# Layer 1 norms with centring and Sqrt, token columns in 4 KB runs, and a layer 3 closed in halves

## The chip, the cores and the metric

The kernel runs on one core of one Trainium2 chip. The metric is the time of one execution on the device in microseconds; it is given as the median of several runs with the lowest and the highest. The profile shows one execution: TensorE (PE, with its weight loads as PEld), VectorE (DVE), ScalarE (ACT), GpSimd (POOL), the sync engine (SP), and the DMA queues. Everything is fp32.

## The reference

The input x is a batch of B = 4 images of 64 x 64 pixels with C = 64 channels. Four layers follow each other:

```python
# layer 0: attention over the N = 4096 pixels of an image
q, k, v = x @ Wq + bq, x @ Wk + bk, x @ Wv + bv
attn = softmax(q @ k.T);  x = gamma * (attn.T @ v) + x
# layer 1: a gated convolution block, with two layer norms over the channels
y = ln(x, ln1_g, ln1_b);  y = dw3x3(y @ pw1_w + pw1_b);  y = y1 * y2      # halves of the channels
y = y * (mean(y over pixels) @ sca_w + sca_b)
x = x + (y @ pw2_w + pw2_b) * beta
z = ln(x, ln2_g, ln2_b) @ pw3_w + pw3_b;  x = x + ((z1 * z2) @ pw4_w + pw4_b) * gamma
# layer 2: attention without weights: rows h are the channels, (w, c) the 4096 tokens
x = x + softmax-weighted sum of x, scores x.T @ x
# layer 3: attention with 32 inner channels, then a batch norm over all images
y = softmax(theta(x) @ phi(x).T) @ g(x)
w_y = y @ w_W + w_b
x = x + gamma3 * (w_y - mean(w_y)) * rsqrt(var(w_y) + 1e-3) + beta3       # mean, var over b, h, w
```

The layer norm is `(x - mean) * rsqrt(var + 1e-6) * g + b` over the 64 channels of a pixel. The batch norm's mean and variance need all four images, so no output can be written before layer 3 of the last image is done.

## The kernel before

**Layout.** An image is held as a tile of 128 partitions x 2048 columns in X. The partitions are (s, c): one of two neighbouring image columns, and the channel. The 2048 columns are blocks q of 128, each (p, h): one of two, and the image row. It comes from DRAM through `fetch_x` (L738): four DMAs an image, each 64 partitions (h) x 8 blocks q x 128 elements (w, c), then eight transposes on TensorE for each half (`load_x`, L923). In `by_rows` (L735) the image's 64 columns are read as (q p w), so that a run in DRAM is 128 elements, 512 bytes. The last loop writes the output with the same view.

**Buffers.** PSUM has three tiles "ps" of 128 x 1024 (`new_ps`), which scores, projections, norms and transposes share, and two accumulators "acc" of 128 x 512. In SBUF there are six tiles e for exponentials, two scratch tiles t of 128 x 1024, and five big ones.

**Order.** The order of TensorE, ScalarE and VectorE is that of the program, written out by `run` (L1416). The backbone is a list `items`: in layer 0 an item is one block of 128 query rows (four score tiles of 128 x 1024, each of two matmuls side by side, each followed by an Exp on ScalarE with a row sum); in layer 2 it is four score tiles of four matmuls; in layer 3 a score group of four matmuls and two Exps. `due` holds what is to be done at an item: products of the exponentials of the items before (two acc tiles, eight matmuls and two reads by VectorE in layer 0), row sums and their reciprocals, and the closing steps of layer 3. Two lanes, `conv` and `misc`, hold generators: layer 1 of each image runs in `conv`, projections and layout changes in `misc`. Each `yield` gives the microseconds after which the lane's next step may go, and a lane is stepped twice an item, ahead of the due work and after it. So layer 1 of image b is spread over the items of layer 0 of image b + 1, and that of the last image over layer 2.

**The norm** (`norm`, L1061, twice an image, eight times in all). The weights pw1 and pw3 are multiplied in `setup` by the gain g and by `cmat`, the matrix I - 1/64 in each half (L907 to L912), so that x need not be centred. The norm takes squares of x on ScalarE (L1066), sums x and its squares over the channels with `jsel` in four 32-column matmuls each (L1072), forms the variance (L1077, L1078), takes Ln and Exp(-0.5 x) of it (L1079, L1080), spreads the result over the partitions with `bsel` (L1086), and multiplies x by it (L1091). Ln, Exp, Square, Identity and Copy are in one set of ScalarE's tables, which L1417 loads once.

**Layer 3** (L1311). The denominators are sums over 32 tiles of exponentials per half image nb. VectorE adds them into esum (L1347, L1349), but every tenth tile is summed by TensorE with `ones` (L1342). `totals` (L1354) sums esum with `ones`, copies z out of PSUM (L1361), takes the reciprocal (L1362) and multiplies (L1363). `close` (L1365) projects with `wo` (L1373), adds the bias on ScalarE (L1375) and takes statistics (L1377) and the extremes of the reciprocals (L1379).

**The end** (from L1447). The aggregate of the statistics (L1454), a matmul with `half` for the mean (L1456), small VectorE steps, a second matmul for the variance (L1463), Ln and Exp (L1465, L1466), scale and shift; then eight rounds of scale (L1476), add (L1477), eight transposes (L1480), two copies (L1484, L1485) and two stores (L1487).

Of the kernel before, what the change touches and what calls it, by code (L numbers as in the profile page):

```python
# [8 lines left out]
F32 = mybir.dt.float32  # L9
AF = mybir.ActivationFunctionType  # L10
# [681 lines left out]
def fast_path(ctx: ExitStack, tc: tile.TileContext, a: dict, out: bass.AP, bad):  # L692
# [16 lines left out]
    PW = 65  # L709
# [25 lines left out]
    by_rows = "h (q p w) c -> p h q (w c)"  # L735
    rows_x = []

    def fetch_x(b, queues):  # L738
        if b % 2 == 0:
            fetch_x.both = new_big("xr")  # L740
        t = fetch_x.both[:, bass.ts(b % 2, 2048)].rearrange("p (q n) -> p q n", n=128)
        src = a["x"][b].rearrange(by_rows, p=2, w=2)
        for g in range(2):
            for p in range(2):
                queues[g].dma_start(
                    out=t[64 * p : 64 * p + 64, bass.ts(g, 8)], in_=src[p, :, bass.ts(g, 8)]
                )
        rows_x.append(t)
# [114 lines left out]
    ones = const.tile([128, 64], F32, name="ones")  # L863
# [21 lines left out]
    def setup():  # L885
        nc.vector.tensor_add(cmat, cmat, ident)
        nc.vector.tensor_scalar_mul(jsel, sel[:, 0:32], 1.0 / C)
        ps = new_ps()
        nc.tensor.transpose(ps[:, 0:128], sel, ident)
        nc.tensor.transpose(ps[:, 512 : 512 + n_rows], rows, ident[:n_rows, :n_rows])  # L890
        nc.vector.tensor_copy(bsel, ps[:, 0:128])
        nc.vector.tensor_copy(vec, ps[:, 512 : 512 + n_rows])
        yield 5.0

        ps = new_ps()
        for i, (w_, sh, bi) in enumerate(
            ((pw1, "L1_conv_ln1_b", "L1_conv_pw1_b"), (pw3, "L1_conv_ln2_b", "L1_conv_pw3_b"))
        ):
            for r in range(2):
                mm(  # L900
                    ps[:, 2 * i + r : 2 * i + r + 1], w_[0:64, bass.ts(r, 128)], V(sh, 0, 0, 64),
                    start=True, stop=True,
                )
            nc.vector.tensor_add(
                pwb[:, i, :], ps[:, 2 * i : 2 * i + 2], vec[:, col[bi] : col[bi] + 2]
            )

        ps = new_ps()
        for i, (w_, g) in enumerate(((pw1, "L1_conv_ln1_g"), (pw3, "L1_conv_ln2_g"))):
            nc.vector.tensor_scalar_mul(w_, w_, V(g))  # L910
            mm(ps[:, 512 * i : 512 * i + 256], cmat, w_, start=True, stop=True)
            nc.vector.tensor_copy(w_, ps[:, 512 * i : 512 * i + 256])  # L912
        nc.vector.tensor_mul(resb[:, 0:1], V("L1_conv_pw2_b"), V("L1_conv_beta"))
        nc.vector.tensor_mul(resb[:, 1:2], V("L1_conv_pw4_b"), V("L1_conv_gamma"))
        yield 3.0
# [5 lines left out]
    bst = const.tile([128, B, 2, 2, 6], F32, name="bst")  # L921
# [139 lines left out]
    def norm(x, y):  # L1061


        sq = [new_t("sq"), new_t("sq")]
        for i in range(2):
            act(sq[i], x[:, bass.ts(i, 1024)], AF.Square)  # L1066
        yield 4.0
        ps = new_ps()
        for i, src in enumerate(((x, x), (sq[0], sq[1]))):
            for j in range(4):  # L1070
                c = 512 * j if i == 0 else 512 * (j % 2)
                mm(  # L1072
                    ps[32 * j : 32 * j + 32, bass.ts(i, 512)], jsel, src[j // 2][:, c : c + 512],
                    start=True, stop=True,
                )
        t = new_t()
        act(t[:, 0:512], ps[:, 0:512], AF.Square)  # L1077
        stt(t[:, 0:512], t[:, 0:512], -1.0, ps[:, 512:1024], ALU.mult, ALU.add)  # L1078
        act(t[:, 0:512], t[:, 0:512], AF.Ln, bias=eps1)  # L1079
        act(t[:, 512:1024], t[:, 0:512], AF.Exp, scale=-0.5)  # L1080
        yield 7.0
        for jp in range(2):
            ps = new_ps()
            for i in range(2):
                p = 32 * (2 * jp + i)
                mm(  # L1086
                    ps[:, bass.ts(i, 512)], bsel[p : p + 32, :], t[p : p + 32, 512:1024],
                    start=True, stop=True,
                )
            cols = bass.ts(jp, 1024)  # L1090
            nc.vector.tensor_mul(y[:, cols], ps, x[:, cols])  # L1091
            yield 3.5

    def layer1(b):
        x = X[:, b]
        y = xn.tile([128, 2048], F32, tag="xn", name="xn")
        yield from norm(x, y)
        yg = new_big("yg")[:, 0:N].rearrange("p (w h) -> p w h", h=H)
        ysum = sm.tile([128, 4], F32, tag="ysum", name="ysum")
        for r in (1, 0):  # L1100
# [6 lines left out]
            inner = pad[:, PW + 1 : 65 * PW + 1].rearrange("p (q s h) -> p q s h", s=2, h=PW)  # L1107
            for j in range(4):
# [6 lines left out]
                for s in range(2):  # L1115
                    act(  # L1116
                        inner[:, bass.ts(j, 8), s, 0:H],
                        ps[:, bass.ts(s, 512)].rearrange("p (q h) -> p q h", h=H),
                        AF.Identity, bias=pwb[:, 0, r : r + 1],
                    )  # L1120
# [24 lines left out]
        pw2s = sm.tile([128, C], F32, tag="pw2s", name="pw2s")  # L1145
        nc.vector.tensor_scalar_mul(pw2s, pw2, ch)
        yield 3.5
        for j in range(4):
            ps = new_ps()
            for s in range(2):  # L1150
                w0 = 16 * j + s
                mm(  # L1152
                    ps[64 * s : 64 * s + 64, 0:512], pw2s, yg[:, w0 : w0 + 15 : 2, :],
# [8 lines left out]
        yield from norm(x, z)  # L1162
# [148 lines left out]
    def layer3(b):  # L1311
        m, first = im[b], len(items)
# [15 lines left out]
        def products(n):  # L1328
# [9 lines left out]
            if mc % 10 == 9:  # L1338
# [15 lines left out]
        def totals():  # L1354
# [6 lines left out]
            nc.scalar.copy(yz[:, 512:1024], z)  # L1361
            nc.vector.reciprocal(yz[:, 512:1024], yz[:, 512:1024])  # L1362
            nc.vector.tensor_mul(yz[:, 0:512], yz[:, 0:512], yz[:, 512:1024])  # L1363

        def close(nb):  # L1365
# [6 lines left out]
            for jj in range(2):  # L1372
                mm(ps[:, bass.ts(jj, 512)], wo[jj], yz[:, 0:512], start=True, stop=True)  # L1373
            wy = wys[b][:, bass.ts(nb, 1024)]
            act(wy, ps, AF.Identity, bias=V("L3_conv_w_b"))  # L1375
            for i in range(2):
                nc.vector.bn_stats(bst[:, b, nb, i, :], wy[:, bass.ts(i, 512)])  # L1377
# [38 lines left out]
    def run():  # L1416
        nc.scalar.preload_act_table_set("natural_log_exp_and_others")  # L1417
# [29 lines left out]
    half = new_t("half")[:, 0:128]  # L1447
    for i in range(2):
        nc.vector.tensor_scalar_mul(half[:, 64 * i : 64 * i + 64], ident[:, 0:64], 0.5)
    for i in range(2):  # L1450
        cols = slice(64 * i, 64 * i + 64)
        stt(half[:, cols], ident[:, 64:128], 0.5, half[:, cols], ALU.mult, ALU.add)
# [3 lines left out]
    mm(ps[:, 0:1], half, mv[:, 0:1], start=True, stop=True)  # L1456
    mean = sm.tile([128, 1], F32, tag="mean", name="mean")
    nc.vector.tensor_copy(mean, ps[:, 0:1])
    dm = sm.tile([128, 1], F32, tag="dm", name="dm")
    nc.vector.tensor_sub(dm, mv[:, 0:1], mean)  # L1460
    nc.vector.tensor_mul(dm, dm, dm)
    nc.vector.tensor_add(dm, dm, mv[:, 1:2])
    mm(ps[:, 512:513], half, dm, start=True, stop=True)  # L1463
    scale = sm.tile([128, 1], F32, tag="scale", name="scale")
    act(scale, ps[:, 512:513], AF.Ln, bias=eps3)  # L1465
    act(scale, scale, AF.Exp, scale=-0.5)  # L1466
    nc.vector.tensor_mul(scale, scale, V("L3_conv_gamma"))
    shift = sm.tile([128, 1], F32, tag="shift", name="shift")
    nc.vector.tensor_mul(shift, scale, mean)
    nc.vector.tensor_sub(shift, V("L3_conv_beta"), shift)  # L1470
    for b in range(B):
        dst = out[b].rearrange(by_rows, p=2, w=2)
# [87 lines left out]
```

## Time and profile before

| what | value |
|---|---|
| time, median of 3 runs | 2802.37 us (2800.41 to 2804.61) |
| the profiled execution's own time | 2800.41 us |
| its span | 2798.1 us |
| TensorE busy | 2710.0 us, 97% |
| ScalarE busy | 1728.7 us, 62% |
| VectorE busy | 1404.0 us, 50% |
| GpSimd busy | 21.6 us, 1% |
| DMA packets | 18500, of these 18181 under 2 KB; 11.80 MB |
| granted TensorE clock, mean | 0.988 |

Busy time is the union of the instructions' times; matmuls are pipelined, and their ends are modelled. A row of the groups reads: line of the kernel, engine, operation, what it writes <- what it reads, the shape out <- in, count; then busy time in us and the mean of one instruction in ns; then the idle time of the engine just ahead of these instructions and what ended it. A row of the order of time begins with the start and the duration in us; the bracket at its end is the idle time before it and what ended that.

### The profile page before, as it was taken

The page shows a single profiled execution, that of the slowest core. Times are in us where ns is not written, and L with a number is a line of the kernel's source. Part 1 is how long each engine was busy: PE and PEld are TensorE (multiplying, and loading weights), DVE is VectorE, ACT ScalarE, POOL GpSimd, SP SyncE. Part 2 cuts the span into 40 slices and gives each one's busy share as a digit, 9 for nine tenths or more (in the row PEclk, how much of TensorE's full clock was granted, in tenths as well). Part 3 has the DMA queues.
Part 4 walks back from the last instruction along what each step waited for, and adds up shares of the span by engine and source line. Part 5 has one row for each costly group of instructions (what it writes and reads, how often), then busy time and mean ns, then how long its engine had stood idle before and what let it go on. Part 6 is the DMA issues. An engine that isn't in the chain of part 4 may idle for free.

```text
span 2798.1 us, 41578 instructions
## 1 busy us (share of the span) xinstructions
PE 2710.0 (97%) x17954; PEld 929.3 (33%) x17954; DVE 1404.0 (50%) x1538; ACT 1728.7 (62%) x2807; POOL 21.6 (1%) x77
## 2 busy tenths in 40 slices
PE   8999999999999899989999999999999999999995
PEld 3343333333333333323333332333322333322222
DVE  2232579338763478126630038810068600298996
ACT  4545555565565565556646568746578655678884
POOL 2000000000000000000000000000000000000000
PEclk9999999999999999999999999999999999999996
DMA  4000000000000000000000000000000000000002
GB/s 70 0 1 1 1 1 1 1 1 1 1 1 0 1 1 1 1 1 1 1 1 1 1 1 1 1 1 1 1 1 1 1 1 1 1 1 1 1 1 62
DMA packets 18500, 11.80 MB, mean 4 GB/s; under 512 B 1436, under 2 KB 18181, under 8 KB 18309
## 3 DMA queue, kind: packets, MB, share of 16 engines
q1 hardware_dynamic: 16085, 7.89, 1.3%
q8 instruction: 142, 2.33, 0.4%
q0 software_dynamic: 928, 0.62, 0.1%
q10 hardware_dynamic: 1296, 0.56, 0.1%
q14 instruction: 49, 0.40, 0.0%
HBM read 4.87 MB, written 4.19 MB: 3 GB/s over the span
## 4 chain that ended last, share of the span: by engine, by line
PE 90%; DVE 6%; ACT 3%; issue 1%; DMA 0%; SPq 0%; ACTq 0%; DVEq 0%
PE acc L1040 16%; PE ps L1016 16%; PE acc L1231 16%; PE ps L1214 15%; PE ps L1321 9%; PE acc L1334 8%; PE ps L1168 2%; DVE tg L1349 1%; PE ps L1111 1%; ACT e L1326 1%; DVE yz L1362 1%; PE accz L1342 1%; PE ps L1373 1%; PE ps L1086 1%; PE ps L1152 1%
## 5 line engine op out<-in xcount | busy, mean ns | idle before, releaser
L1020 ACT ACTIVATE e<-ps 128x1024 f32<-128x1024 f32 x512 | 517.1, 1025 | 328.2 <-PE ps L1016 202.3
L1222 ACT ACTIVATE e<-ps 128x1024 f32<-128x1024 f32 x512 | 517.1, 1025 | 322.3 <-PE ps L1214 322.1
L1326 ACT ACTIVATE e<-ps 128x1024 f32<-128x1024 f32 x512 | 496.0, 1022 | 110.1 <-PE ps L1321 95.1
L1349 DVE TENSOR_TENSOR tg<-tg,e 128x2048 f32<-128x2048 f32 x216 | 495.0, 2291 | 26.2 <-ACT e L1326 7.7
L1016 PE MATMUL ps<-X,q 64*128 64x512 f32 x2048 | 490.3, 606 | 15.2 <-ACT ko L1197 7.0
L1214 PE MATMUL ps<-ko 64*64 64x512 f32 x4096 | 471.7, 595 | 16.3 <-ACT ko L1197 13.3
L1231 PE MATMUL acc<-e,X 64*64 64x512 f32 x4096 | 469.5, 593 | 2.7 <-DVE X L1047 2.1
L1040 PE MATMUL acc<-e,vq 128*64 128x512 f32 x2048 | 468.0, 599 | 0.0
L1321 PE MATMUL ps<-tg,ph 32*128 32x512 f32 x2048 | 320.5, 640 | 5.6 <-ACT e L1326 4.2
L1047 DVE SCALAR_TENSOR_TENSOR yv<-acc,gam,yv 128x512 f32<-128x512 f32 x224 | 167.9, 750 | 274.3 <-PE acc L1040 262.5
L1016 PEld LDWEIGHTS ps<-X,q 64*128 64x128 f32 x2048 | 190.6, 187 | 295.1 <-issue 186.6
L1334 PE MATMUL acc<-e,tg 128*32 128x512 f32 x2048 | 272.4, 604 | 1.3 <-ACT yz L1352 1.3
L1214 PEld LDWEIGHTS ps<-ko 64*64 64x64 f32 x4096 | 156.8, 133 | 302.9 <-issue 193.5
L1231 PEld LDWEIGHTS acc<-e,X 64*64 64x64 f32 x4096 | 160.4, 133 | 282.1 <-issue 266.8
L1040 PEld LDWEIGHTS acc<-e,vq 128*64 128x64 f32 x2048 | 136.5, 137 | 311.4 <-issue 290.4
L1239 DVE TENSOR_TENSOR ph<-ph,acc 128x512 f32<-128x512 f32 x16 | 11.0, 688 | 429.4 <-ACT ph L1238 429.4
L1321 PEld LDWEIGHTS ps<-tg,ph 32*128 32x128 f32 x2048 | 102.3, 182 | 223.5 <-issue 149.9
L1133 DVE SCALAR_TENSOR_TENSOR yg<-pad,vec,yg 128x1024 f32<-128x1024 f32 x128 | 164.3, 1283 | 5.3 <-ACT pad L1116 1.8
L1133 DVE SCALAR_TENSOR_TENSOR y<-pad,vec,y 128x1024 f32<-128x1024 f32 x128 | 164.3, 1284 | 3.7
L1020 ACT ACTIVATION_READ_ACCUMULATOR e<-ps 128x1 f32 x512 | 106.2, 208 | 0.0
L1222 ACT ACTIVATION_READ_ACCUMULATOR e<-ps 128x1 f32 x512 | 106.1, 207 | 0.0
L1334 PEld LDWEIGHTS acc<-e,tg 128*32 128x32 f32 x2048 | 41.0, 108 | 194.9 <-issue 189.2
(178 smaller groups left out, 1132.4 us busy)
## 6 DMA issues: line engine op xcount, KB each, us to landing
out_dram<-o SPq DMA_DIRECT2D x16, 256.0 KB
xr<-in_x_dram SPq DMA_DIRECT2D x14, 256.0 KB
xr<-in_x_dram ACTq DMA_DIRECT2D x2, 256.0 KB
pw<-in_L_conv_pw_w_dram POOLq DMA_DIRECT2D x4, 64.0 KB, 4.8
phw<-in_L_conv_phi_W_dram POOLq DMA_DIRECT2D x8, 8.0 KB, 1.8
sca<-in_L_conv_sca_w_dram POOLq DMA_DIRECT2D x1, 64.0 KB, 6.2
pw<-in_L_conv_pw_w_dram POOLq DMA_DIRECT2D x2, 32.0 KB, 4.9
thw<-in_L_conv_theta_W_dram POOLq DMA_DIRECT2D x4, 8.0 KB, 1.9
```

The costliest lines, as they stand in the source:

```text
L1016: mm(ps[:, bass.ts(r, 512)], m.q[rows_, bass.ts(t, 128)], x[rows_, bass.ts(g, 512)], start=True, stop=True,)
L1020: act(es[g // 2][:, bass.ts(g % 2, 1024)], ps, AF.Exp, bias=SHIFT0, accum_out=zs[:, g : g + 1],)
L1040: mm(accs[g][64 * r : 64 * r + 64, :], vq, es[half][:, 1024 * g + 512 * r : 1024 * g + 512 * r + 512], start=t == 2 * p, stop=t == 2 * p + 1,)
L1047: stt((x if p == 15 else m.y)[:, cols], accs[g], gam0, (m.y if p else x)[:, cols], ALU.mult, ALU.add,)
L1133: stt(out_, win, wt, out_, ALU.mult, ALU.add)
L1214: mm(ps[64 * c : 64 * c + 64, bass.ts(r, 512)], m.ko[rows_, 128 * jb + 64 * c : 128 * jb + 64 * c + 64], m.ko[rows_, bass.ts(2 * ib + r, 5 ...
L1222: act(es[n, jb], ps, AF.Exp, bias=SHIFT2, accum_out=m.zs[:, jb, ib : ib + 1])
L1231: mm(acc[r][64 * c : 64 * c + 64, :], xw[rows_, jb, :], es[n, jb][rows_, bass.ts(c, 512)], start=jb == 0, stop=jb == 31,)
L1321: mm(tiles[k // 2][:, bass.ts(k % 2, 512)], m.ph[rows_, bass.ts(mc, 128)], m.th[rows_, bass.ts(nb, 512)], start=True, stop=True,)
L1326: act(e[:, bass.ts(kp, 1024)], tiles[kp], AF.Exp)
L1334: mm(st["y"][32 * k : 32 * k + 32, :], m.gx[:, mc, :], e[:, bass.ts(k, 512)], start=mc == 0, stop=mc == 31,)
L1349: nc.vector.tensor_add(esum, esum, e)
```

## The change

Four parts, all within the same function.

- **Columns.** `by_rows` reads the image's columns as (p q w): p now selects a half of the image, q the block within it. The eight blocks q of a DMA then lie next to each other in DRAM, 4 KB. The places where layer 1 turns blocks into image columns (the padded input of the convolution, and the reads of yg for pw2) step accordingly.
- **Norms.** The weights are no longer folded. A norm centres x with `cmat` in two rounds of 1024 columns, on TensorE; ScalarE squares the centred tile out of PSUM, and VectorE copies it to SBUF; `jsel` sums the squares in two pairs into a PSUM tile var, which is held from the first round to the end of the second; Sqrt and VectorE's reciprocal take the place of Ln and Exp; the last product takes g. The yields are 7, 7, 10, 3.5, 3.5 in place of 4, 7, 3.5, 3.5. The early load of the table set is dropped.
- **Layer 3.** In the last image, TensorE sums the last two tiles of exponentials as it does every tenth. `totals` works in halves of 256 columns, and in the last image out of PSUM, with no copy of z; `close` projects, adds the bias and takes statistics in the same halves.
- **Mean and variance.** Both come from one round of matmuls, with a second column block of `half` for the differences; Sqrt and a reciprocal in place of Ln and Exp.

```diff
-    by_rows = "h (q p w) c -> p h q (w c)"
+    by_rows = "h (p q w) c -> p h q (w c)"
...
-        src = a["x"][b].rearrange(by_rows, p=2, w=2)
+        src = a["x"][b].rearrange(by_rows, p=2, q=16)
...
-        ps = new_ps()
-        for i, (w_, g) in enumerate(((pw1, "L1_conv_ln1_g"), (pw3, "L1_conv_ln2_g"))):
-            nc.vector.tensor_scalar_mul(w_, w_, V(g))
-            mm(ps[:, 512 * i : 512 * i + 256], cmat, w_, start=True, stop=True)
-            nc.vector.tensor_copy(w_, ps[:, 512 * i : 512 * i + 256])
...
-    bst = const.tile([128, B, 2, 2, 6], F32, name="bst")
+    bst = const.tile([128, B, 2, 4, 6], F32, name="bst")
...
-    def norm(x, y):
-        sq = [new_t("sq"), new_t("sq")]
-        for i in range(2):
-            act(sq[i], x[:, bass.ts(i, 1024)], AF.Square)
-        yield 4.0
-        ps = new_ps()
-        for i, src in enumerate(((x, x), (sq[0], sq[1]))):
-            for j in range(4):
-                c = 512 * j if i == 0 else 512 * (j % 2)
-                mm(
-                    ps[32 * j : 32 * j + 32, bass.ts(i, 512)], jsel, src[j // 2][:, c : c + 512],
-                    start=True, stop=True,
-                )
+    def norm(x, g, y):
+        var = None
+        for jp in range(2):
+            ps = new_ps()
+            for i in range(2):
+                mm(ps[:, bass.ts(i, 512)], cmat, x[:, bass.ts(2 * jp + i, 512)], start=True, stop=True)
+            t = new_t()
+            act(t, ps, AF.Square)
+            nc.vector.tensor_copy(y[:, bass.ts(jp, 1024)], ps)
+            yield 7.0
+            if var is None:
+                var = new_ps("var")
+            for i in range(2):
+                p = 32 * (2 * jp + i)
+                mm(var[p : p + 32, 0:512], jsel, t[:, bass.ts(i, 512)], start=True, stop=True)
         t = new_t()
-        act(t[:, 0:512], ps[:, 0:512], AF.Square)
-        stt(t[:, 0:512], t[:, 0:512], -1.0, ps[:, 512:1024], ALU.mult, ALU.add)
-        act(t[:, 0:512], t[:, 0:512], AF.Ln, bias=eps1)
-        act(t[:, 512:1024], t[:, 0:512], AF.Exp, scale=-0.5)
-        yield 7.0
+        act(t[:, 0:512], var[:, 0:512], AF.Sqrt, bias=eps1)
+        nc.vector.reciprocal(t[:, 512:1024], t[:, 0:512])
+        yield 10.0
...
-            cols = bass.ts(jp, 1024)
-            nc.vector.tensor_mul(y[:, cols], ps, x[:, cols])
+            ys = y[:, bass.ts(jp, 1024)]
+            stt(ys, ps, g, ys, ALU.mult, ALU.mult)
...
-            inner = pad[:, PW + 1 : 65 * PW + 1].rearrange("p (q s h) -> p q s h", s=2, h=PW)
+            inner = pad[:, PW + 1 : 65 * PW + 1].rearrange("c (p q s h) -> c q p s h", p=2, s=2, h=PW)
...
-                w0 = 16 * j + s
                 mm(
-                    ps[64 * s : 64 * s + 64, 0:512], pw2s, yg[:, w0 : w0 + 15 : 2, :],
+                    ps[64 * s : 64 * s + 64, 0:512], pw2s,
+                    yg.rearrange("c (p q s) h -> c q p s h", p=2, s=2)[:, bass.ts(j, 4), :, s, :],
                     start=True, stop=True,
                 )
...
-            if mc % 10 == 9:
+            if mc % 10 == 9 or (last and n >= 62):
...
-            nc.scalar.copy(yz[:, 512:1024], z)
-            nc.vector.reciprocal(yz[:, 512:1024], yz[:, 512:1024])
-            nc.vector.tensor_mul(yz[:, 0:512], yz[:, 0:512], yz[:, 512:1024])
+            if not last:
+                nc.scalar.copy(yz[:, 512:1024], z)
+                z = yz[:, 512:1024]
+            for i in range(2):
+                cols, inv = bass.ts(i, 256), slice(512 + 256 * i, 768 + 256 * i)
+                nc.vector.reciprocal(yz[:, inv], z[:, cols])
+                nc.vector.tensor_mul(yz[:, cols], yz[:, cols], yz[:, inv])
...
-            for jj in range(2):
-                mm(ps[:, bass.ts(jj, 512)], wo[jj], yz[:, 0:512], start=True, stop=True)
-            wy = wys[b][:, bass.ts(nb, 1024)]
-            act(wy, ps, AF.Identity, bias=V("L3_conv_w_b"))
             for i in range(2):
-                nc.vector.bn_stats(bst[:, b, nb, i, :], wy[:, bass.ts(i, 512)])
+                cols = bass.ts(i, 256)
+                for jj in range(2):
+                    mm(
+                        ps[:, 512 * jj + 256 * i : 512 * jj + 256 * i + 256], wo[jj], yz[:, cols],
+                        start=True, stop=True,
+                    )
...
+                act(
+                    wy, ps.rearrange("p (j n) -> p j n", j=2)[:, :, cols], AF.Identity,
+                    bias=V("L3_conv_w_b"),
+                )
+                for jj in range(2):
+                    nc.vector.bn_stats(bst[:, b, nb, 2 * i + jj, :], wy[:, jj, :])
...
-        nc.scalar.preload_act_table_set("natural_log_exp_and_others")
...
-    mm(ps[:, 0:1], half, mv[:, 0:1], start=True, stop=True)
...
-    mm(ps[:, 512:513], half, dm, start=True, stop=True)
+    mm(ps[:, 0:2], half[:, 0:128], mv, start=True, stop=True)
+    mm(ps[:, 512:513], half[:, 128:256], mv[:, 0:1], start=True, stop=True)
...
-    act(scale, ps[:, 512:513], AF.Ln, bias=eps3)
-    act(scale, scale, AF.Exp, scale=-0.5)
+    act(scale, mean[:, 3:4], AF.Sqrt, bias=eps3)
+    nc.vector.reciprocal(scale, scale)
```

## The prediction

> **What bounds the kernel now.** I read the page first: the busy times, then the chain that ended last.
>
> ```profile
> span 2798.1 us, 41578 instructions
> PE 2710.0 (97%) x17954; PEld 929.3 (33%) x17954; DVE 1404.0 (50%) x1538; ACT 1728.7 (62%) x2807; POOL 21.6 (1%) x77
> PE 90%; DVE 6%; ACT 3%; issue 1%; DMA 0%; SPq 0%; ACTq 0%; DVEq 0%
> ```
>
> TensorE is busy for 97% of the span and carries 90% of the chain; ScalarE and VectorE have room on average. So matmul time added in the middle is added to the end, and work on the other two costs only where TensorE runs into it. The exceptions are the first 15 us and the last 50. Next the groups by form, for the matmuls and the table load that the change touches:
>
> ```profile
> L1072 PE MATMUL ps<-X,jsel 128*32 128x512 f32 x64 | 8.5, 605 | 0.0
> L1072 PE MATMUL ps<-sq,jsel 128*32 128x512 f32 x64 | 8.3, 592 | 0.0
> L1282 PE MATMUL ps<-X,thw 128*128 128x512 f32 x32 | 15.1, 611 | 1.2 <-DVE X L1267 1.2
> L1417 ACT ACT_TABLE_LOAD x1 | 1.3, 1283 | 4.0 <-issue 4.0
> ```
>
> One fp32 matmul is two instructions here: L1282 has 16 matmuls in the code and 32 in the row. Its full 128x128 matmul costs 15.1/16 = 0.94 us. Four 32-column matmuls of L1072 together cost 8.5/8 = 1.06 us, because they run side by side. Then the order of time around the first norm:
>
> ```profile
> 288.58 1.06 PE L1072 MATMUL ps<-X,jsel 128*32 128x512 f32 x8
> 289.46 1.04 PE L1072 MATMUL ps<-sq,jsel 128*32 128x512 f32 x8
> 290.43 2.85 PE L1016 MATMUL ps<-X,q 64*128 64x512 f32 x12
> 290.63 0.60 ACT L1077 ACTIVATE t<-ps 128x512 f32<-128x512 f32 x1 [2.08 <-PE ps L1072]
> 292.80 0.63 ACT L1080 ACTIVATE t<-t 128x512 f32<-128x512 f32 x1
> 294.48 1.13 PE L1016 MATMUL ps<-X,q 64*128 64x512 f32 x4 [1.20 <-ACT e L1020]
> 299.12 1.13 PE L1086 MATMUL ps<-t,bsel 32*128 32x512 f32 x4
> 300.18 3.70 PE L1016 MATMUL ps<-X,q 64*128 64x512 f32 x16
> ```
>
> From start to start the statistics take 290.43 - 288.58 = 1.85 us of TensorE, and a pair of matmuls standing alone takes 300.18 - 299.12 = 1.06. The bracket [1.20] is the norm's one stall: ScalarE is held by the chain L1077 to L1080 until 293.43, so the fourth score tile finds no free buffer. Last, the order of time at the end:
>
> ```profile
> 2712.85 38.23 DVE L1349 TENSOR_TENSOR tg<-tg,e 128x2048 f32<-128x2048 f32 x16
> 2751.13 1.93 PE L1357 MATMUL accz<-tg,ones 128*32 128x512 f32 x8 [5.36 <-DVE tg L1349]
> 2753.75 3.35 DVE L1362 RECIPROCAL yz<-yz 128x512 f32<-128x512 f32 x1 [2.17 <-ACT yz L1361]
> 2757.98 3.75 PE L1373 MATMUL ps<-yz,wo 128*128 128x512 f32 x4 [4.91 <-DVE yz L1363]
> 2765.30 0.58 DVE L1454 BATCH_NORM_AGGREGATE mv<-bst 128x2 f32<-128x96 f32 x1
> 2787.39 0.59 ACT L1485 COPY o<-ps 128x512 f32<-128x512 f32 x1 [2.53 <-DMA out_dram<-o]
> ```
>
> VectorE's running sum is behind (2.39 us an add), then everything is a chain of single steps, and the output loop waits for stores.
>
> **What the Trainium skill says.** "ScalarE: Activation LUTs", Table sets: Exp and Ln share a set, Exp and Sqrt do not, so Exp, Sqrt, Exp is two loads; What ACT_TABLE_LOAD costs: 1283 ns and a drain of 1380. The trace has the 1283 (L1417) and no row for a drain. "TensorE: Matmul & The Clock Gate", Part 3: matmuls on different column strips run together; the 1.06 us for four agrees, and a full matmul has nothing to run beside. "PSUM — Partial Sum Buffer", Terms: two engines may not use one bank at once, reads included, so the norm's Square and copy of one tile go one after the other; no row of before shows such a pair. "DMA: Bandwidth & Descriptors", Specifications: line rate from 512 B up, 27 GiB/s an engine.
>
> **The norms, eight of them.** TensorE loses 1.85 us of statistics. It gains four centring matmuls, 4 x 0.94 = 3.78, and two jsel pairs that now stand apart, 2 x 1.06 = 2.12; the bsel pairs stay. That is 5.90 - 1.85 = +4.05 a norm, 32.4 in all.
>
> ScalarE loses Square, Ln and Exp on 512 columns (0.60 + 0.72 + 0.63, rows L1077, L1079, L1080) and gains Sqrt (as Ln, 0.72) and two loads (2 x 1.28): +1.34. The first load waits for nothing and fits the idle 2.08 us before L1077. Sqrt and the second load hold ScalarE for 2.0 us, where the old chain held it for 293.43 - 290.63 = 2.8. So I cost the loads at nothing; with that cover gone each costs its 1.28.
>
> VectorE loses a 0.69 us combination and two products of 1.22; it gains two copies of 1.22, a reciprocal of 3.35 (as L1362) and two products of 1.28: +5.2 us, on an engine half idle. Queued behind it are the reads of acc (0.75 each), which give TensorE its two acc buffers, and vq, which the next products need. In the worst order vq is late by about 0.6.
>
> The new wait is for ps. There are three such tiles. The var tile holds one from its first pair until Sqrt, a full item, and a centred tile is held through Square (1.03) and copy (1.22), some 2.3 us past its matmuls, where a score tile needs 0.92 of TensorE and 1.0 of Exp. If the step falls ahead of scores, the second score tile waits 2.4 - 0.9 = 1.5 us; ahead of products, which need no ps and last 3.65, about 0.4. Behind a waiting score tile stands all that TensorE has, the item's products first. Half and half gives 1.0 a norm, with the lost stall of 1.20 and the late vq about cancelling. Bounds: -0.6 (only a stall goes) to +2.3 (everything collides). Sum: 8 x 5.05 = 40.4, between 27.6 and 50.8. The longer yields cost nothing: layer 1 then ends some 11 items later, still in layer 2, before layer 3 needs its buffers.
>
> **Start and setup.** Folding the weights goes: in the trace TensorE sits from 46.89 to 49.67 with nothing but L911 to do, 2.8 us. After it the granted clock is 0.91 over 40 to 60 us, and part of that may go: 0.5. Total -3.3 (0 to -4.5). The second group of transposes waits 0.43 for x: -0.4 (0 to -1). The first table load moves behind the same DMA issues, ahead of a copy that starts at 9.68: nothing.
>
> **The end.** Two adds fewer, and VectorE is done at 2751.08 - 2 x 2.39 = 2746.3; TensorE sums those two tiles itself (2 x 0.97), so its last product ends at 2747.7 instead of 2745.77, and the totals begin there: they end at 2748.75, at full clock (1.04 as L1342) instead of 1.93. The copy of z (0.59) goes. Reciprocals and products in halves: 2 x (1.75 + 0.43), from 3.35 and 0.69 by length, to 2753.2. Second half of L1373 by 1.2 (3.75 at half clock is 1.87 a matmul; half the columns, two matmuls, and some of it at full clock), ACT 0.70, two bn_stats of 0.42, the two reductions 1.26, the aggregate 0.6: 2758.1, against 2765.9. That is -7.8. One round for mean and variance saves a matmul round and adds a reciprocal: -0.6, its table load under the wait. Stores: 50.5% of 16 engines over 30 us for 8192 packets is 29.5 ns for 512 B, 17.3 GB/s an engine; the 4 KB packets of the weights ran at 233 ns, 17.6. So the rate hardly grows; fewer packets and 4.0 us of waits in the loop make me take -2 (0, the measured rates; -6, an estimate from the skill's 27 GiB/s: 9 us for 4.19 MB against 15). Together -10.4 (-6 to -14). The column order itself, in pads, yg and pw2s reads, moves the same elements: nothing.
>
> **Sum.** +40.4 - 3.3 - 0.4 - 10.4 = +26.3 on the profiled execution's 2800.4 (span 2798.1 and 2.3 around it): 2826.7. The median of the runs is 2.0 above that execution: 2829.
>
> **Rivals.** (A) Loads and reciprocals are not covered: 16 loads at 1.28 on the path add 20.5, 2849. For it: ScalarE feeds every score tile and var leaves it two. Against: the idle 2 to 4 us before its waits. (B) Faster, one mechanism: the centring matmuls fill gaps of TensorE that its modelled ends hide, so a norm costs nothing: 2802.4 - 14.1 = 2788. It decides from a norm's cost below 14.1/8 = 1.8 us. For it: busy time here is modelled. Against: score tiles follow each other at 0.92 without a gap, and the statistics took 1.85 from start to start. (C) Half of that: a full matmul in a run costs 0.86, no ps wait is added and the old stall goes, so a norm costs 3.1 and the end gives 14: 24.8 - 17.7 = +7, 2809. For it: matmuls in long runs start every 0.43 an instruction.
>
> **Chances.** Main 0.62 (2814 to 2842 alone), A 0.16, B 0.09, C 0.13. A measurement of this kernel can tell about 0.2%, 5.6 us, from no change. Slower has the main case, A and most of C: 0.86; same a little of C: 0.05; faster B: 0.09. The range leaves out B and the upper part of A: 2806 to 2850.
>
> **What would show it.** Sixteen more table loads and one for the end; the centring row at 0.9 us a matmul; idle time of L1016 and L1214 before ACT and DVE of 5 to 15 us more; the aggregate 10 us after layer 3's last product (L1334) instead of 19.5; TensorE's busy time up by some 30. I am wrong if that busy time hardly moves, if the loads stand in the chain, or if the stores end much sooner.

## The result, and the profile after

| what | before | after |
|---|---|---|
| time, median of 4 runs each | 2802.72 us (2800.41 to 2804.61) | 2837.88 us (2831.36 to 2839.92) |
| ratio, 95% interval | | 1.0122 (1.0104 to 1.0140) |
| profiled execution, its span | 2800.41, 2798.1 us | 2831.36, 2829.5 us |
| TensorE busy | 2710.0 us | 2747.0 us |
| DMA packets | 18500 | 4165 |

The kernel is slower by 35.2 us by the medians, and by 31.0 in the two profiled executions, of which that of after is the fastest of its four. The page of the changed kernel, the lines that answer to those of before:

```profile
span 2829.5 us, 41733 instructions
...
PE 2747.0 (97%) x17998; PEld 933.9 (33%) x17998; DVE 1442.9 (51%) x1584; ACT 1747.4 (62%) x2813; POOL 21.6 (1%) x77
...
PE 91%; DVE 4%; ACT 3%; issue 1%; DMA 0%; ACTq 0%; POOL 0%; DVEq 0%; POOLq 0%
```

TensorE gained 37 us of work at the same 97%, so it still sets the time. Its groups by form, and those of ScalarE and VectorE that the norm brought (last fields: busy us, mean ns of one, idle time before and what ended it):

```profile
L1061 PE MATMUL ps<-X,cmat 128*128 128x512 f32 x64 | 31.7, 618 | 0.0
...
L1070 PE MATMUL var<-t,jsel 128*32 128x512 f32 x64 | 16.8, 605 | 0.0
...
L1073 DVE RECIPROCAL t<-t 128x512 f32<-128x512 f32 x8 | 26.8, 3353 | 52.1 <-ACT t L1072 52.1
...
L1072 ACT ACT_TABLE_LOAD x8 | 10.3, 1283 | 7.0 <-PE var L1070 6.8
...
L1372 PE MATMUL ps<-yz,wo 128*128 128x256 f32 x64 | 23.8, 508 | 10.6 <-ACT wy L1377 7.1 <-DVE yz L1360 3.5
```

The centring matmuls are 0.99 us each (31.7/32). The last row is one that the prediction didn't look for: the closes of layer 3 wait 7.1 us for ScalarE's step L1377. The order of time through the second half of the first norm:

```profile
287.08 1.05 PE L1070 MATMUL var<-t,jsel 128*32 128x512 f32 x4
...
288.06 1.98 PE L1061 MATMUL ps<-X,cmat 128*128 128x512 f32 x4
...
289.98 1.13 PE L1010 MATMUL ps<-X,q 64*128 64x512 f32 x4
...
290.08 1.02 ACT L1063 ACTIVATE t<-ps 128x1024 f32<-128x1024 f32 x1 [5.39 <-PE ps L1061]
...
291.14 1.22 DVE L1064 COPY xn<-ps 128x1024 f32<-128x1024 f32 x1 [2.64 <-ACT t L1063]
...
292.42 1.99 PE L1010 MATMUL ps<-X,q 64*128 64x512 f32 x8 [1.31 <-DVE xn L1064]
...
299.40 1.05 PE L1070 MATMUL var<-t,jsel 128*32 128x512 f32 x4
...
300.57 1.28 ACT L1072 ACT_TABLE_LOAD   x1 [3.52 <-PE var L1070]
...
301.86 0.69 ACT L1072 ACTIVATE t<-var,eps 128x512 f32<-128x512 f32 x1
...
302.57 1.28 ACT L1014 ACT_TABLE_LOAD   x1
...
303.87 1.02 ACT L1014 ACTIVATE e<-ps 128x1024 f32<-128x1024 f32 x1
...
305.03 1.13 PE L1010 MATMUL ps<-X,q 64*128 64x512 f32 x4 [1.30 <-ACT e L1014]
```

Square and copy of one PSUM tile run one after the other, and the second score tile waits 1.31 us for the copy: the predicted wait for ps. The first table load doesn't run ahead of its Sqrt: it stands behind the wait for var (3.52), so load, Sqrt and load hold ScalarE from 300.57 to 303.85, and the fourth score tile waits another 1.30. Next a close of layer 3 at full clock, the second of image 0:

```profile
1890.32 1.13 PE L1372 MATMUL ps<-yz,wo 128*128 128x256 f32 x4
...
1891.94 0.71 ACT L1377 ACTIVATE wy<-ps,vec 128x512 f32<-128x512 f32 x1
...
1892.70 1.13 PE L1372 MATMUL ps<-yz,wo 128*128 128x256 f32 x4 [1.25 <-ACT wy L1377]
...
1893.77 2.81 PE L1224 MATMUL acc<-e,X 64*64 64x512 f32 x24
```

It holds TensorE from 1890.32 to 1893.77, 3.44 us. The same close of the kernel before took 1.91:

```profile
1859.29 1.98 PE L1373 MATMUL ps<-yz,wo 128*128 128x512 f32 x4
...
1861.20 3.66 PE L1231 MATMUL acc<-e,X 64*64 64x512 f32 x32
```

And the end of the changed kernel:

```profile
2778.12 9.48 DVE L1342 TENSOR_TENSOR tg<-tg,e 128x2048 f32<-128x2048 f32 x4
...
2789.73 1.04 PE L1350 MATMUL accz<-tg,ones 128*32 128x512 f32 x8
...
2790.84 1.76 DVE L1359 RECIPROCAL yz<-accz 128x256 f32<-128x256 f32 x1 [2.28 <-PE accz L1350]
...
2795.39 1.54 PE L1372 MATMUL ps<-yz,wo 128*128 128x256 f32 x4 [1.09 <-DVE yz L1360]
...
2799.54 1.01 DVE L1459 BATCH_NORM_AGGREGATE mv<-bst 128x2 f32<-128x192 f32 x1
...
2803.40 5.77 ACT L1479 ACTIVATE wy<-wy,shift,scale 128x1024 f32<-128x1024 f32 x5 [0.87 <-DVE shift L1473]
...
2818.30 0.59 ACT L1488 COPY o<-ps 128x512 f32<-128x512 f32 x1 [1.19 <-DVE o L1487]
```

Where the 31.4 us of span went, by the same step in both traces: up to the ninth item of layer 0, -3.4; from there to the first scores of layer 3, where all norms are, from -3.4 to +27.0, so +30.4; layer 3 to its last scores, from +27.0 to +42.4, so +15.4; the end, from +42.4 to +31.4, so -11.0.

The stretch of the norms can be taken apart. From start to start, L1061 and L1070 hold TensorE for 30.6 + 15.7 us where L1072 held it for 14.8: +31.5. The idle times of TensorE around the eight norms sum to 11.8 against 6.9: +4.9. The pads cost 2.1 (experiment 4). On the other side, two waits of TensorE for `ko`, the tile that layer 2's scores read, are shorter. Before, and then after:

```profile
968.80 1.22 PE L1016 MATMUL ps<-X,q 64*128 64x512 f32 x2 [6.80 <-ACT ko L1197]
...
1261.38 1.13 PE L1214 MATMUL ps<-ko 64*64 64x512 f32 x4 [7.78 <-ACT ko L1197]
```

```profile
968.01 1.13 PE L1010 MATMUL ps<-X,q 64*128 64x512 f32 x4 [3.63 <-ACT ko L1190]
...
1250.05 1.99 PE L1207 MATMUL ps<-ko 64*64 64x512 f32 x8 [3.12 <-ACT ko L1190]
```

That is -7.8. Before, VectorE ran convolution steps of layer 1 (2.60 and 3.92 us of L1133) ahead of its copies of `ko`; with the new norm layer 1 runs later and has none there. All seven kernels with the new norm show the shorter waits, all seven with the old one the longer. Last, the half clock: the profile lists stretches in which TensorE was granted half of its clock, three of 20.4 us in all before (from 963.8, 1257.4 and 1581.7), one of 3.4 after (1249.7), in part while TensorE waits anyway. The matmuls that started in them took 5.6 us longer before, and 1.6 after, than the same kinds at full clock: -4.1, an estimate from these means. The sum is +26.6 of the 30.4 seen; the other 3.8 is spread, most of it over score matmuls that start a little later, and isn't explained.

### The profile page after: what moved, and what is told of

It is laid out like the page before. It is cut to its first block, busy times and chain, and to the rows that moved or that the text cites. A ratio compares the mean times of both kernels' runs of the same rounds, so it can differ in the third digit from the quotient of the medians.

```text
span 2829.5 us, 41733 instructions
## 1 busy us (share of the span) xinstructions
PE 2747.0 (97%) x17998; PEld 933.9 (33%) x17998; DVE 1442.9 (51%) x1584; ACT 1747.4 (62%) x2813; POOL 21.6 (1%) x77
## 2 busy tenths in 40 slices
DMA packets 4165, 11.81 MB, mean 4 GB/s; under 512 B 1436, under 2 KB 1797, under 8 KB 3973
## 4 chain that ended last, share of the span: by engine, by line
PE 91%; DVE 4%; ACT 3%; issue 1%; DMA 0%; ACTq 0%; POOL 0%; DVEq 0%; POOLq 0%
PE acc L1034 16%; PE ps L1010 16%; PE acc L1224 16%; PE ps L1207 15%; PE ps L1314 10%; PE acc L1327 8%; PE ps L1161 2%; PE ps L1104 1%; PE ps L1061 1%; ACT e L1319 1%; ACT e L1215 1%; PE accz L1335 1%; DVE yz L1359 1%; PE ps L1372 1%; PE ps L987 1%
## 5 line engine op out<-in xcount | busy, mean ns | idle before, releaser
L1014 ACT ACTIVATE e<-ps 128x1024 f32<-128x1024 f32 x512 | 517.2, 1024 | 342.6 <-PE ps L1010 234.3
L1215 ACT ACTIVATE e<-ps 128x1024 f32<-128x1024 f32 x512 | 517.3, 1024 | 313.7 <-PE ps L1207 313.2
L1010 PE MATMUL ps<-X,q 64*128 64x512 f32 x2048 | 491.4, 605 | 13.4 <-ACT e L1014 4.2
L1342 DVE TENSOR_TENSOR tg<-tg,e 128x2048 f32<-128x2048 f32 x214 | 490.4, 2292 | 26.1 <-ACT e L1319 8.1
```

The costliest lines, as they stand in the source:

```text
L1010: mm(ps[:, bass.ts(r, 512)], m.q[rows_, bass.ts(t, 128)], x[rows_, bass.ts(g, 512)], start=True, stop=True,)
L1014: act(es[g // 2][:, bass.ts(g % 2, 1024)], ps, AF.Exp, bias=SHIFT0, accum_out=zs[:, g : g + 1],)
L1215: act(es[n, jb], ps, AF.Exp, bias=SHIFT2, accum_out=m.zs[:, jb, ib : ib + 1])
L1342: nc.vector.tensor_add(esum, esum, e)
```

## The experiments

The main theory: matmuls given to TensorE are paid in full, a norm's other steps cost little beyond two waits, and two things were missed, the closes in halves and the pads. Rivals: the table loads are on the path; the halves cost clock or instructions, not a wait; the columns pay in the output loop. Each kernel was timed beside the kernel before on the same chip (2801.3 to 2802.0 us by its medians); the changed kernel's 2837.9 is from the four runs above, so a difference to it of a few us is no more than a hint.

**1. The norm alone.** The change's part "Norms" (new `norm`, no folded weights, no early table load, and one buffer for pw2s, as in the changed kernel); everything else as before.

> Only the norm of layer 1 is changed (with the folding of the weights gone and the early table load gone); columns, closes and end are those of before. Theory: the norms cost 4.9 us each (39 in all) and setup gives 3.3 to 4.4 back, so about +35 us: 2838 us, ratio 1.0126 (1.0105 to 1.0140). Rival, the centring matmuls fall into gaps of TensorE and the other parts make the kernel slow: +5 or less, ratio at most 1.002. Rival, half the cost: +15 to +20.

Measured: 2831.86 us, ratio 1.0104 (1.0088 to 1.0119), +29.9. The ratio is just under the range. The rows and stalls of the norms are those of the changed kernel (31.7 us of L1061, 11.8 us of idle time), and so are the two shorter waits for `ko`, which the expectation didn't have. Its profiled execution is the slowest of its four, with a span 34.9 above that of before: 30.8 of this lies between the ninth item and layer 3, where the changed kernel has 30.4; the setup gives 0.9 there instead of 3.4, and layer 3 and the end cost 3.6 and 1.4. The norm is the larger part of the 35 us, and by itself a loss.

**2. Is the added matmul work paid in full?** The centring matmuls issued twice:

```diff
-                mm(ps[:, bass.ts(i, 512)], cmat, x[:, bass.ts(2 * jp + i, 512)], start=True, stop=True)
+                for _ in range(2):
+                    mm(ps[:, bass.ts(i, 512)], cmat, x[:, bass.ts(2 * jp + i, 512)], start=True, stop=True)
```

> The changed kernel with every centring matmul issued twice into the same tile (32 matmuls of 128x512 more in all; the result is the same). Theory, TensorE is the bound and a matmul that it is given there costs what it takes from start to start, 30.6 us for the 32 of the changed kernel: 27 to 33 us above the changed kernel, 2865 to 2871 us. Rival, gaps of TensorE hide such matmuls: under 10 us above it.

Measured: 2863.59 us, ratio 1.0224 (1.0210 to 1.0238), 25.7 above the changed kernel by the medians, a little short of the 27 to 33. Its group row:

```profile
L1062 PE MATMUL ps<-X,cmat 128*128 128x512 f32 x128 | 59.2, 605 | 0.0
```

From start to start these now hold 58.1 us, 27.5 more, and between the ninth item and layer 3 its trace falls 30.7 us behind the changed kernel's, of which some 3.4 us are one more half-clock stretch of 6.8 (at 985; half of it, an estimate): about 27.3 at equal clock. The idle time around the norms is 11.8 again. So the matmuls are paid in full, and no gap hides them. A matmul added to a run costs 0.86 (27.5/32); in the changed kernel's pairs, which stand apart from their kind, one costs 0.96 (30.6/32).

**3. The waits within the norm.** Ln and Exp(-0.5) in place of Sqrt and reciprocal, with the early table load back, which takes 16 table loads away:

```diff
-        act(t[:, 0:512], var[:, 0:512], AF.Sqrt, bias=eps1)
-        nc.vector.reciprocal(t[:, 512:1024], t[:, 0:512])
+        act(t[:, 0:512], var[:, 0:512], AF.Ln, bias=eps1)
+        act(t[:, 512:1024], t[:, 0:512], AF.Exp, scale=-0.5)
```

> The changed kernel with Ln and Exp at -0.5 in the norm in place of Sqrt and reciprocal: no table load in layers 1 to 3. Theory, loads are hidden but for the 0.5 us by which ScalarE is held longer: 0 to 6 us below the changed kernel, 2832 to 2838 us. Rival A, both loads of each norm lie on the path: 16 x 1.28 = 20 us below it, 2817 us.

Measured: 2832.26 us, ratio 1.0103 (1.0088 to 1.0118), -5.6 by the medians, though the two kernels' intervals overlap. The trace says more: the idle time around the norms falls from 11.8 to 8.7 us, 1.5 in each of two norms:

```profile
298.73 3.73 PE L1010 MATMUL ps<-X,q 64*128 64x512 f32 x16
...
298.93 0.69 ACT L1072 ACTIVATE t<-var,eps 128x512 f32<-128x512 f32 x1 [3.53 <-PE var L1070]
...
299.65 0.63 ACT L1073 ACTIVATE t<-t 128x512 f32<-128x512 f32 x1
```

All eight score matmuls of the item (16 instructions) now run in one piece. In the six other norms of the changed kernel TensorE has an item's products next, 3.65 us that need no ps, and no idle time shows behind the loads there. Rival A, 20 us, is out.

The second wait: VectorE's copy first, and Square from the copy, so that the ps tile is free after one read:

```diff
-            act(t, ps, AF.Square)
             nc.vector.tensor_copy(y[:, bass.ts(jp, 1024)], ps)
+            act(t, y[:, bass.ts(jp, 1024)], AF.Square)
```

> The changed kernel with VectorE's copy of a centred tile first and ScalarE's Square taken from the copy, so the ps tile is free after one read (1.2 us) instead of two (2.3 us). Theory, the score tile's wait of 1.3 us for that tile is what a norm costs beyond its matmuls: about 1 us a norm, 5 to 10 us below the changed kernel, 2828 to 2833 us. Rival, the wait is moved to the next tile or to Square: within 3 us of it.

Measured: 2835.59 us, ratio 1.0121 (1.0106 to 1.0137): no difference that can be told. The order of time at the same place:

```profile
293.32 1.13 PE L1010 MATMUL ps<-X,q 64*128 64x512 f32 x4
...
293.42 1.23 DVE L1063 COPY xn<-ps 128x1024 f32<-128x1024 f32 x1 [1.58 <-PE ps L1061]
...
294.68 1.06 ACT L1064 ACTIVATE t<-xn 128x1024 f32<-128x1024 f32 x1 [5.37 <-DVE xn L1063]
...
294.70 1.13 PE L1010 MATMUL ps<-X,q 64*128 64x512 f32 x4 [0.26 <-DVE xn L1063]
...
296.80 2.13 PE L1010 MATMUL ps<-X,q 64*128 64x512 f32 x8 [0.96 <-ACT e L1014]
```

The wait of 1.31 is down to 0.26, but Square, now behind the copy, keeps ScalarE from the first Exp until 295.64, and the next tile waits 0.96. The theory fell here: with one read instead of two the wait moved to the next score tile, which needs an Exp that Square now holds up on ScalarE. Both orders have waits of this kind in three of the eight norms alone; the other five show 0.36 to 0.38 each.

**4. The columns.** The change's part "Columns" alone: `by_rows` and the steps that write pads and read yg.

> The kernel before with the column layout of loads and stores alone. Theory: the output loop ends 3 to 4 us sooner after its first scaling, the start is within 1 us: -2 to -4 us, ratio 0.9986 to 0.9993. Rival, the rate of the transfers sets the loop and not the number of packets: within 1 us of before. Rival, the strided reads of pads and gated tiles on the engines cost something: above before.

Measured: 2803.68 us, ratio 1.0010 (1.0004 to 1.0017), +2.4: the second rival. The output loop takes as long as before from the first scaling to the last copy (+0.1), and the stores behind it end 0.9 sooner. But between the ninth item and layer 3 the trace falls back by 2.7 us: 2.1 of it at twelve places, 0.13 to 0.20 each, where score tiles stand behind a step that writes a pad, 0.4 at the end of a half-clock stretch that both kernels have, and 0.2 spread. ScalarE's instructions of the pad line, of the kernel before and then of the one with the columns, and last a pair of them in the order of time of the latter. The three durations of a row are the shortest, the median and the longest in ns:

```profile
L1116 ACT ACTIVATE pad<-ps,pwb x64: 686/690/744, 306.1 to 1319.3; 128x512 f32<-128x512 f32 x64
L1116 ACTq EVENT_SEMAPHORE  x8: 17/28/4403, 306.0 to 1299.9; - x8
```

```profile
L1116 ACT ACTIVATE pad<-ps,pwb x64: 687/695/717, 305.1 to 1321.5; 128x512 f32<-128x512 f32 x64
L1116 ACTq EVENT_SEMAPHORE  x32: 17/17/4407, 305.1 to 1320.1; - x32
```

```profile
309.77 1.41 ACT L1116 ACTIVATE pad<-ps,pwb 128x512 f32<-128x512 f32 x2 [3.23 <-PE ps L1111]
```

The instructions are as long as before, but there are 24 more semaphore waits, and a pair takes 1.41 where it took 1.28 (310.69 to 311.97 before): the second no longer starts under the first, in any of the 32 pairs. The rows of the two steps lie between each other in both layouts; in the new one each step also reaches into both halves of the tile. That they therefore count as overlapping is my reading; the added waits and the 0.13 are seen.

**5. The closes in halves.** `totals` and `close` whole in the first seven blocks, in halves only in the last. The edit of `close` (`totals` has the same):

```diff
-            for i in range(2):
-                cols = bass.ts(i, 256)
+            parts = 2 if last and nb else 1
+            for i in range(parts):
+                n = 512 // parts
+                cols = bass.ts(i, n)
```

> The changed kernel with totals and close in halves in the very last of the eight blocks alone, the other seven whole as before. Theory: a close in halves holds TensorE 1.5 to 2.9 us longer than a whole one, since its second half waits until ScalarE has read the first out of the same tile, and three of the seven drop to half clock: 14 to 18 us below the changed kernel, 2820 to 2824 us. Rival, the lost time comes back elsewhere: within 4 us of the changed kernel, 2834 to 2842.

Measured: 2823.3 us, ratio 1.0081 (1.0067 to 1.0095), 14.6 below the changed kernel. The seven closes hold TensorE for 16.3 us where they held it for 27.8 (13.4 before). What in them costs it is told by moving the second half's matmuls ahead of ScalarE's first step:

```diff
             for i in range(2):
                 cols = bass.ts(i, 256)
                 for jj in range(2):
                     mm(...)
+            for i in range(2):
+                cols = bass.ts(i, 256)
                 wy = ...
```

> The changed kernel with the four projection matmuls of both halves of a close issued ahead of ScalarE's two steps; totals and closes stay in halves. Theory, the cost of the halves is the wait of the second half's matmuls for ScalarE: it goes, a close holds TensorE about 2 us as before, and the time falls by 11 to 15 us, as with whole closes: 2823 to 2827 us. Rival, smaller matmuls, twice the steps on ScalarE and VectorE, or a drop of the granted clock that the halves bring with them cost it: within 4 us of the changed kernel, 2834 to 2842.

Measured: 2826.89 us, ratio 1.0090 (1.0076 to 1.0104), 11.0 below the changed kernel, at the edge of the theory's range. The same close as above:

```profile
1893.62 1.99 PE L1372 MATMUL ps<-yz,wo 128*128 128x256 f32 x8
...
1895.54 2.81 PE L1224 MATMUL acc<-e,X 64*64 64x512 f32 x24
```

It takes 1.92 us, as a whole one. So smaller matmuls and more steps cost TensorE nothing; the wait for ScalarE's read of the shared tile is the cost, 1.4 to 1.5 us at each close at full clock, some 10 us for seven. Two halves in separate PSUM tiles were not tried. The first closes of images 0 to 2 also ran at half clock: 4.7 to 4.9 us in the changed kernel, but 3.4 to 3.6 with the matmuls ahead, and 3.4 to 3.6 with whole closes and the new norm (experiment 1). The half-clock stretches there last 6.8 us in the changed kernel and 3.4 in these two: the halves with their wait make them longer, but don't bring them. So of the 14.4 us by which the seven closes grew, the part beyond some 10 lies at half clock.

**6. The parts of the end.** The last two sums on TensorE alone, then one round for mean and variance alone:

> The kernel before with the last two sums of the last block on TensorE alone; VectorE drops two adds there. Theory, the totals begin 3.4 us sooner and run at 1.04 in place of 1.93 us: -3.4 to -4.7, about 2797.5 us. Rival, the part of the end behind it is slower for a lower clock or a later VectorE: -2 or less.

> The kernel before with one round for mean and variance alone (Sqrt and reciprocal at the end, its table load with it). Theory: in the kernels with that part the adds and copies of the output loop follow each other in another order on VectorE and ScalarE, and from the first scaling to the last copy they take 2.9 to 3.7 us less; 0.7 more comes from the round itself, and the last stores give up to 1.2 back: -2.5 to -4, about 2798.5 us. Rival, the loop is shorter because of the 4 KB stores: -0.7, within 1.5 us of before.

Measured: 2796.77 us, ratio 0.9986 (0.9979 to 0.9992), -4.8; and 2799.15 us, ratio 0.9991 (0.9983 to 1.0000), -2.4, at the edge of its range and hardly clear of no change. With the last sums the totals begin 3.8 us sooner and end 4.7 sooner. With one round the first scaling comes 0.7 sooner and the last copy another 3.0, with no change of layout; but the stores end 9.9 us behind the last copy instead of 8.1, so 1.9 of this is lost again. The output loop of that kernel:

```profile
2769.62 3.50 DVE L1476 TENSOR_TENSOR X<-X,wy 128x1024 f32<-128x1024 f32 x3 [1.31 <-ACT wy L1475]
...
2773.04 0.68 DVE L1483 COPY o<-ps 128x512 f32<-128x512 f32 x1
...
2773.64 1.22 DVE L1476 TENSOR_TENSOR X<-X,wy 128x1024 f32<-128x1024 f32 x1
...
2774.77 0.68 DVE L1483 COPY o<-ps 128x512 f32<-128x512 f32 x1
```

VectorE does add, copy, add, copy, where the kernel before did three copies and then three adds (the second row of adds at 2777.60, 3.48 us). Code behind `run` is not ordered by hand; the planner that orders it when the kernel is built gave the loop another order when the steps ahead of it changed. All kernels here with one round have adds and copies mixed like this, and none without; why the planner does so isn't shown.

**7. What is worth keeping.** The norm of before, the last sums, one round for mean and variance, and halves in the last block alone (as in experiment 5); with the columns, and without them. Where the norm of before meets the larger bst, four tiles of a few bytes (mv, mean, scale, shift) have one buffer instead of two, to fit.

> The changed kernel with the norm of before and with halves in the last block alone; columns, last sums on TensorE and one round for mean and variance as changed. Theory, the costs of the norm (30 to 35 us) and of the seven closes (14 to 15 us) and the gain of the end (11 us) simply add: 8 to 12 us below the kernel before, ratio 0.9957 to 0.9971. Rival, the gains of the end depend on the delay before it: within 4 us of before.

> The kernel before with last sums on TensorE, halves in the last block alone and one round for mean and variance; norm and columns as before. Theory, the column layout costs 2.7 us in the steps that write the pads (1.41 in place of 1.28 us for a pair of ScalarE steps in front of score tiles) and gives about 0.9 back behind the last copy: 1 to 2.5 us below the kernel that has the layout besides, 2792 to 2794 us, ratio to before about 0.9968. Rival, the layout is worth its 3 to 4 us in the output loop: above that kernel, 2797 to 2799.

Measured: 2794.86 us, ratio 0.9973 (0.9964 to 0.9982), 6.5 below the kernel before and so short of the 8 to 12; and 2791.98 us, ratio 0.9970 (0.9958 to 0.9982), at the edge of its range. Both beat the kernel before and the changed one, by 0.3% in the case of the former. Without the layout it is 2.9 us less by the medians; the two intervals overlap, but the sign is that of experiment 4. With the columns, and halves in all eight blocks (the changed kernel with the norm of before):

> The changed kernel with the norm of before (weights folded again, early table load kept); columns, halves, last sums and mean and variance as changed. Theory: start and end give 11 to 12 us and the seven closes in the middle of layer 3 cost 14 to 18 in halves, so +2 to +7 against before: 2805 to 2810 us. Rival, the closes cost nothing by themselves (what they lose in time they give back in granted clock): -9 to -12, 2791 to 2794 us.

Measured: 2808.2 us, ratio 1.0018 (1.0011 to 1.0025), 13.3 above the same kernel with halves in the last block alone.

By the medians the parts add up: norm with setup +29.9, columns +2.4, halves in seven closes +14.6, the end without columns -9.6 (2791.98 against 2801.59): +37.3, against 35.2 measured. Each of these differences is uncertain by 2 to 6 us.

## Why the prediction was right, and where it was wrong

Forecast 2829, measured 2837.9, slower as said. Its signs came: 17 more table loads, TensorE busy for 37 us more, the aggregate 10.5 us after layer 3's last product. The sign and most of the size have the cause that was given; that the sum came within 9 us is in part luck, since two costs were missing (+16.5), and so were two gains (-7.8 at the waits for `ko`, -4.1 at half clock).

- **"+4.05 a norm, 32.4 in all"**: right. 31.5 from start to start, and experiment 2 shows that such work is paid. This refutes rival B, which lived on gaps, and C, which put a norm at 3.1: start to start alone is 3.9.
- **"Half and half gives 1.0 a norm"**: the mechanism is right (1.31 at the score tile, 0.36 ahead of products), the share was wrong. Three norms of eight meet scores, and the net of all stalls is 4.9 us, not 8. The prediction also took the freeing of the tile for the whole of the wait; experiment 3 shows ScalarE's time behind it.
- **"The first load waits for nothing and fits the idle 2.08 us"**: wrong in two of the eight norms, where it stands behind the wait for var; in the other six it starts 0.02 us behind the step before it. In the two, ScalarE is held 3.3 us where 2.0 were said, and this costs 1.5 us each, 3.1 in all. So costing the loads near nothing held, for the reason given under rival A's "against" less than for the order of the items: mostly products come next. The Trainium skill's page "ScalarE: Activation LUTs", What ACT_TABLE_LOAD costs, adds a drain of 1380 ns; Exp starts at 303.87, 0.02 us behind its load, so no second 1.38 is seen.
- **The Trainium skill's page "PSUM — Partial Sum Buffer", Terms**: that two engines' reads of one tile go one after the other agrees: Square ends at 291.10 and the copy starts at 291.14. The copy waits there for a semaphore (2.64 "<-ACT t L1063"), so the program itself has this order, and no run shows what would happen without it.
- **Setup, "-3.3 (0 to -4.5)"**: -3.4 in the profiled execution. The six other kernels above with the changed setup stand between -5.1 and -0.1 at the ninth item, those with the old one between -1.0 and +1.5, so the size can't be told better than that.
- **The change to `close` was costed in the last block alone.** This is the step that failed: the sum has the halves' gain at the end and no term for the seven closes in the middle, where the same code runs with TensorE as the bound. What they show: +14.4 us from start to start, 14.6 by experiment 5, some 10 of it the second half's wait for ScalarE.
- **"The column order itself ... nothing"**: wrong. It moves the same elements, but the two pad writes of a step no longer overlap: +2.1.
- **The end, "-10.4"**: -11.0. Up to the aggregate -7.75 (said: -7.8), mean and variance -0.7 (said: -0.6), loop and stores -2.5 (said: -2). The last was right in size and in part wrong in its cause, which was the packets alone. From the first scaling to the end of the stores the kernel before takes 28.6 us, one round alone 27.5 (the new order saves 3.0 in the loop, the stores give 1.9 back), the columns alone 27.8, and the changed kernel, with both, 26.1.
- **"The longer yields cost nothing"**: they brought something. Layer 1 runs later, and the two waits for `ko` are 7.8 us shorter.
- **"The median of the runs is 2.0 above that execution"**: it is 6.5 above (2837.88 against 2831.36). The profiled execution of the changed kernel had a granted clock of 0.992, the three others 0.990. So its small loss to half clock is in part its own, and about half of the 9 us that the forecast missed lies here.

## What to carry to other kernels

When one function serves the middle and the end, cost an edit in both: splitting a step shortens a chain at the end, but where TensorE is the bound, two halves that share one PSUM tile put another engine's read between its matmuls, unless all matmuls are issued first. Price added matmuls from start to start in the trace, in full, and look for what comes next on TensorE (scores or products) to tell which waits count. A step that runs later can shorten a wait elsewhere, so look at what shared the engines with it before. A layout that makes transfers longer runs can cost more on the engines that write it than the transfers give back.

## What the hardware showed that was not expected

- A table load can stand behind a wait of the activation that needs it, and then idle time ahead of that wait doesn't hide it. In the first norm a wait of Sqrt is an instruction of its own (EVENT_SEMAPHORE, at 300.50) ahead of the load, which starts at 300.57 after 3.52 us of idle time. Where the activation carries the wait itself, the load ran ahead of it: at the end the load starts at 2797.68, and its Sqrt only at 2802.24; behind six of the eight Sqrts, Exp starts 1.02 to 1.21 us after its load has ended.
- Two ScalarE writes of one tile lost their overlap when the layout of the rows changed: 24 more semaphore waits, which the program sets, 1.41 us a pair instead of 1.28.
- Stores in runs of 4 KB instead of 512 B (experiment 4 against before): a mean busy share of 0.67 over 21.6 us against 0.69 over 22.4, so 14.5 us of transfer against 15.5, 18 GB/s an engine against 17.
- TensorE is granted half clock in stretches of about 3.4 us and multiples, also in the middle, where it is 97% busy. They sum to 46 us after the first 40 in the profiled execution of the changed kernel and 72 in that of before; 22 and 45 of these lie behind the last scores, where TensorE mostly waits. In the 14 traces, all 70 stretches between 100 us and the last scores begin during an idle time of TensorE of 0.7 us or more, or at most 1.7 us behind one; but most such idle times bring none (the 3.63 us ahead of 968.01 in the changed kernel, for one), and what decides stays open.
- The spread between runs of one kernel goes with the granted clock. Of the 18 runs of the changed kernel with the norm of before, the four at 0.991 took 2802 to 2805 us, the eleven at 0.987 and 0.988 took 2807 to 2811. This is as large as several parts of the change, and a reason to compare clocks before durations.
